# Splitting a turn of six PSUM banks into four and two in a decoder kernel

## The chip, the core and the metric

The kernel runs on one core of a Trainium2 chip. [...] TensorE's results land in PSUM, which has eight banks of 128 partitions by 512 single-precision numbers. A bank can be written again only when the last reader of its old contents is done. The metric is the device time of one execution in microseconds (us): less is better.

## What is computed

The reference is one decoder layer on x of shape (4, 256, 512) with a context of shape (4, 1601, 512):

```python
x = _layernorm(x + _L0_attn_ref(x, ...))        # attention over the 16 head dimensions, per position
x = _layernorm(x + _L0_xattn_ref(x, context))   # cross attention, most of the work
x = _layernorm(x + _L0_ffn_ref(x, ...))         # softmax router, top 8 of 64, mixes expert biases

def _L0_xattn_ref(latents, context, Wq, Wk, Wv, Wo, q_norm_w, k_norm_w):
    kv = concatenate([context, latents], axis=1)           # 1601 + 256 rows
    q, k, v = latents @ Wq, kv @ Wk, kv @ Wv               # 32 query heads, 8 key/value heads, 128 wide
    q, k = rms_norm(q, q_norm_w), rms_norm(k, k_norm_w)
    probs = softmax(q @ k.T / sqrt(128))                   # 4 query heads share one key/value head
    return concat(probs @ v) @ Wo
```

## The kernel before

**Precision.** Each large operand is kept as a high and a low half-precision part, and each product is three matmuls: high by high, high by low, low by high (`mm3`, lines 229 to 235; the three matmuls are lines 233, 234 and 235).

**Tiling.** The 1857 rows of keys and values of a sequence lie in 15 tiles of 128 (the last has 65 rows), taken in eight pairs. A unit is one key/value head of one sequence: 8 heads by 4 sequences give 32 units, and sequence 0's eight units come first. A unit has four query heads, so there are 128 heads in all. The text calls such a query head a head, and its place in the schedule is a number: head n stands at n.

**One unit.** `kv_proj` (line 382) projects one pair onto keys and values, 24 matmuls into one PSUM bank named `kvp`. ACT squares the keys and sums the squares (line 395), POOL turns the sums into factors (397, 398), ACT and DVE make the high and low part of the values (403, 404). Later `kv_n` (408) reads the same bank again to scale the keys (ACT 418, DVE 420), which ends the bank's use, and `kv_tr` transposes the keys with a transfer. `q_proj` (432) does the same for the queries of one row tile, four heads at once, into a bank named `qp`; `q_n` (447, DVE line 451) ends its use. All this is done for the next unit while the four heads of the present one are worked through:

- `qk` (476): six matmuls make one bank `s` of scores. ACT copies it out (490), DVE takes a running maximum from it (494, 496, 499).
- `qmax`, `qmax_t`, `qmax_b`: maximum over all keys, through a bank of its own (`mt`).
- `soft` (532): for each of four chunks, DVE subtracts the maximum (537), ACT makes the exponential twice, in half and in single precision (540, 541), POOL subtracts the two for the low part (542). Eight buffers hold scores, five hold probabilities.
- `pv` (544): probabilities by values, lines 561 to 563, into one accumulator bank `o`.
- `oevac` (566): DVE and ACT empty that bank (571, 578, 580).
- `wout` (597): product with Wo into a bank `wo`, added to the result by DVE (608).

**Banks.** Six of the eight banks are one pool, `psu` (line 75), for `s`, `kvp`, `qp`, `wo` and all other matmul outputs and transposes of single-precision tiles; the maximum (`psm`) and the accumulator (`psv`) have one each.

**Order.** The opening, up to the keys and queries of the first two units, is a list written out by hand, `START` (line 29): `load`, `make`, `keep` are the context's load, its transposition and split, and its copy to memory; `proj`, `norm`, `turn` are the steps of a pair for units 0 and 1 both; `qproj`, `qnorm`, `qturn` those of unit 0's queries; `a0`, `a1`, `x0`, `x1` the steps of the first attention layer's two row tiles; `lw1`, `w1` its weights; `wkv`, `wkw`, `lwq`, `wq` weights of the second layer, `skv`, `skw`, `sq` their copies. From line 699 on every step gets a position, mostly a multiple of head numbers plus a constant from the table `AT` (line 38), and the steps are emitted by position. So `exp` and `exps` place the four chunks of `soft`, `evac` places `oevac` after a head's first `pv`, and `norm` and `turn` place `kv_n` and `kv_tr` after `kv_proj`, in parts of one tenth of the unit. Units 0 to 7 also split and save their weights (`wprep`); between sequences there are the first layer of the next one (`stage1`) and the router stage of the last one (`stage3`).

The tile framework then plans each engine's queue at compile time: it takes the emitted order as priority, and where a step's inputs or its bank would not be ready in its plan, later steps of the same engine go first. A bank of a pool is given to whichever tile the plan has next. The trace shows it: among 1108 allocations between 490 and 2322 us, 177 began while the tile six allocations earlier still held its bank.

Of the kernel before, what the change touches and what calls it, by code (L numbers as in the profile page):

```python
# [10 lines left out]
F32 = mybir.dt.float32  # L11
# [4 lines left out]
PSUM = bass.MemoryType.PSUM  # L16
DRAM = bass.MemoryType.DRAM

P = 128
# [7 lines left out]


START = """
    a0 x0 lw1 load1 w1 make1 load0 wkw wkv make0 x1 load2 a0 lwq2 a0 keep0 load3 a0 proj0 a1 norm0 a1 proj1 a1  # L30
    norm1 load4 turn1 make2 a1 load5 proj2 make3 norm2 proj3 turn0 lwq0 a0 keep1 load7 a0 norm3 a1 skv a0 a1
    make4 a1 a1 proj4 keep3 turn2 wq0 keep2 a0 make5 make7 a0 keep5 proj5 proj7 norm4 a1 wq2 turn4 make6 skw
    qproj0 norm7 qnorm0 norm5 keep6 qproj1 keep7 keep4 turn5 turn3 qturn0 proj6 qnorm1 sq qturn1 turn7 norm6
    turn6
"""


AT = dict(maxt=0.13, maxb=0.229, exp=0.327, exps=0.2, pv=2.184, pvs=-2.469, evac=1.148, out=3.37, wout=4.006, wouts=-0.187,
          qk=-0.206, qmax=-0.269, norm=0.859, turn=1.093, lead=2.991, span=3.805, z0=2, z1=1, wkv=7.932, wq=5.971,
          wqs=0.513, wq1=4.753, wo0=3.105, wo=0.635, bkv=9.366, bq=5.482, bo=3.236, lq1=2.103, l1lo=-1.004,  # L40
          l1b=-24.402, l1w=-1.49, srcl=0.764, mklo=1.584, mkb=-23.779, mke=-2.064, mktl=-1.781, prep3=3.694, s3=5.382,
          s3i=-0.465, s3w=3.874, s3l=-0.111, s3lw=0.484, lw1=2.586, lw2=3.64, lmaxt=0.127, lmaxb=0.286, lexp=0.335,
          lexps=0.178, lpv=2.055, levac=1.151, lout=3.348, lqk=1.003, lqkw=0.833)

@with_exitstack
def tile_decoder(ctx: ExitStack, tc: tile.TileContext, x, cx, Wq1, bq1, Wk1, bk1, Wv1, bv1,
# [9 lines left out]
    G = Wq.shape[1] // Wk.shape[1]  # L56
# [15 lines left out]
    pS = ctx.enter_context(tc.tile_pool(name="pS", bufs=8))  # L72
    pP = ctx.enter_context(tc.tile_pool(name="pP", bufs=5))
    dr = ctx.enter_context(tc.tile_pool(name="dr", bufs=1, space=DRAM))
    psu = ctx.enter_context(tc.tile_pool(name="psu", bufs=6, space=PSUM))
    psm = ctx.enter_context(tc.tile_pool(name="psm", bufs=1, space=PSUM))
    psv = ctx.enter_context(tc.tile_pool(name="psv", bufs=1, space=PSUM))

# [150 lines left out]
    def mm3(dst, quads, start=True, stop=True, skip=False):  # L229

        n = len(quads)
        for k, (ah, al, bh, bl) in enumerate(quads):
            nc.tensor.matmul(dst, ah, bh, start=start and k == 0, stop=False, skip_group_check=skip)  # L233
            nc.tensor.matmul(dst, ah, bl, start=False, stop=False, skip_group_check=skip)  # L234
            nc.tensor.matmul(dst, al, bh, start=False, stop=stop and k == n - 1, skip_group_check=skip)  # L235
# [4 lines left out]
    def wprep_kv(h):  # L240
        s = pst.tile([P, NC, 2 * P], F32, tag="st", name=f"st_kv_{h}")
        nc.sync.dma_start(out=s[:, :, 0:P], in_=Wk[:, h * P:(h + 1) * P].rearrange("(c p) d -> p c d", p=P))
        nc.sync.dma_start(out=s[:, :, P:], in_=Wv[:, h * P:(h + 1) * P].rearrange("(c p) d -> p c d", p=P))
        w = Wt["kv", h] = p2.tile([P, 2, NC, 2 * P], F16, tag="wkv", name=f"wkv_{h}")
        split(w[:, 0], w[:, 1], s, WS)
        if h >= HB:
            wsave("kv", h)
# [52 lines left out]
    def nk(t):  # L300
        return REM if t == NT - 1 else P

    def kview(tile_, t):

        o = (t % 2) * 2 * NC * P
        return tile_[:, o:o + 2 * NC * P].rearrange("p (l c k) -> p l c k", l=2, c=NC)[:, :, :, :nk(t)]

    def tiles_of(p):
        return [t for t in (2 * p, 2 * p + 1) if t < NT]
# [72 lines left out]
    def kv_proj(u, p):  # L382
        h, b = units[u]
        wkv = Wt["kv", h]
        ts_ = tiles_of(p)
        n = len(ts_)
        k = nk(ts_[0])
        ps = psu.tile([P, 2, 2 * P], F32, tag="u", name=f"kvp_{u}_{p}")
        for j, t in enumerate(ts_):
            v = kview(kvt[u, p], t)  # L390
            mm3(ps[:k, j, :], [(v[:, 0, c], v[:, 1, c], wkv[:, 0, c], wkv[:, 1, c]) for c in range(NC)])
        ss = p2.tile([P, 2], F32, tag="kss", name=f"kss_{u}_{p}")
        kn = p2.tile([P, 2, P], F32, tag="kn", name=f"kn_{u}_{p}", bufs=2)
        for j in range(n):
            nc.scalar.activation(kn[:k, j, :], ps[:k, j, 0:P], AF.Square, accum_out=ss[:k, j:j + 1])
        rk = p2.tile([P, 2], F32, tag="krk", name=f"krk_{u}_{p}")
        nc.gpsimd.tensor_scalar(ss[:k, :n], ss[:k, :n], 1.0 / (P * QS * QS), 1e-6 * PW * PW / (QS * QS), ALU.mult, ALU.add)
        nc.gpsimd.tensor_tensor(rk[:k, :n], ss[:k, :n], mhalf[:k, :n], ALU.pow)
        v = NPAIR * u + sum(q[0] == u for q in vuse.values())
        assert v < VR or ("pv", *vuse[v - VR]) in done  # L400
        vuse[v] = (u, p)
        vh, vl = VT[u, p] = vring[v % VR]
        nc.scalar.activation(vh[:k, :n, 0:P], ps[:k, :n, P:], AF.Copy, scale=VS / PW)
        nc.vector.scalar_tensor_tensor(vl[:k, :n, :], ps[:k, :n, P:], VS / PW, vh[:k, :n, 0:P],
                                       ALU.mult, ALU.subtract)
        kns[u, p] = (kn, rk, ps)
# [25 lines left out]
    def q_proj(u, i):  # L432
        h, b = units[u]
        wq = Wt["q", h]
        ps = psu.tile([P, G, P], F32, tag="u", name=f"qp_{u}_{i}")
        v = kview(kvt[u, TL], NF + i)
        mm3(ps.rearrange("p g d -> p (g d)"), [(v[:, 0, c], v[:, 1, c], wq[:, 0, c], wq[:, 1, c]) for c in range(NC)])
        ss = p2.tile([P, G], F32, tag="qss", name=f"qss_{u}_{i}")
        qn = p2.tile([P, G, P], F32, tag="qn", name=f"qn_{u}_{i}", bufs=1)
        for g in range(G):  # L440
            nc.scalar.activation(qn[:, g, :], ps[:, g, :], AF.Square, accum_out=ss[:, g:g + 1])
        rq = p2.tile([P, G], F32, tag="qrq", name=f"qrq_{u}_{i}")
        nc.gpsimd.tensor_scalar(ss, ss, 1.0 / P, 1e-6 * PW * PW, ALU.mult, ALU.add)
        nc.gpsimd.tensor_tensor(rq, ss, mhalf[:, :G], ALU.pow)
        qns[u, i] = (qn, rq, ps)
# [182 lines left out]
    def stage3(b, i):  # L628
# [14 lines left out]
        for c in range(NC):  # L643
# [31 lines left out]
    x0 = [stage1(0, i) for i in range(NQ)]  # L675
    first = dict(x0=lambda: next(x0[0]), x1=lambda: next(x0[1]), lw1=prep1_load, w1=prep1,
                 wkv=lambda: wprep_kv(0))
    for i in range(NQ):
        first[f"a{i}"] = lambda i=i: next(x0[i], None)
        first[f"lwq{2 * i}"] = lambda i=i: wload_q(0, 2 * i)  # L680
        first[f"wq{2 * i}"] = lambda i=i: wprep_q(0, 2 * i)
        for k, f in (("qproj", q_proj), ("qnorm", q_n), ("qturn", q_tr)):
            first[f"{k}{i}"] = lambda f=f, i=i: f(0, i)
# [4 lines left out]
    for p in range(NPAIR):  # L688
        for k, f in (("load", src_load), ("make", kv_make), ("keep", lambda b, p: kv_keep(b, p, kvt[b, p]))):
            first[f"{k}{p}"] = lambda f=f, p=p: f(0, p)  # L690
        for k, f in (("proj", kv_proj), ("norm", kv_n), ("turn", kv_tr)):
            first[f"{k}{p}"] = lambda f=f, p=p: [f(u, p) for u in range(HB)]
# [14 lines left out]

    A = AT
    WOUT = A["out"] + A["wout"]
# [30 lines left out]
    for u in range(U):  # L740
        h, b = units[u]
        if u > 0:
            t0 = 4 * (u - 1)
            if u > 1:
                at(t0 - 0.01, proj_new, u)
            steps = [("kv", p) for p in range(NPAIR) if p != TL]
            z = A["z0"] if h == 0 else A["z1"]
            steps[z:z] = [("kv", TL), ("q", 0), ("q", 1)]
            if u == 1:
                steps = [("q", 0), ("q", 1)] + 8 * [("", 0)]  # L750
            step = A["span"] / len(steps)
            for k, (what, v) in enumerate(steps):
                pos = t0 + step * k
                norm, turn = min(pos + A["norm"] * step, 4 * u - 0.006), min(pos + A["turn"] * step, 4 * u - 0.005)
                if what == "kv" and u > 1:
                    at(pos - A["lead"] * step, kv_load, u, v)
                    at(pos, kv_proj, u, v)
                    at(norm, kv_n, u, v)
                    at(turn, kv_tr, u, v)
                elif what == "q":  # L760
                    at(pos, q_proj, u, v)
                    at(norm, q_n, u, v)
                    at(turn, q_tr, u, v)
# [58 lines left out]
```

## Time and profile before

| | us |
|---|---|
| median of 3 runs | 2449.8 |
| lowest and highest | 2444.4, 2451.77 |
| profiled execution | 2446.54 |
| its span, first to last instruction | 2444.8 |
| TensorE busy | 2360.6 |
| ScalarE busy | 2082.2 |
| VectorE busy | 1919.7 |
| GpSimd busy | 1500.9 |

The profile is of one execution. Busy time counts an engine's instructions without those of its sequencer. Matmuls overlap in the array, so their ends are modelled. A line of waits names the waiting engine, the tile and line it was about to write, and who released it, then the sum in us, the number of times and the longest. In groups of instructions `out<-in` names what is written and read, then partitions by elements. The granted clock of TensorE is a share of full speed.

In the trace the first matmul starts at 6.2 us, the context's first transposition at 15.06 us, the first scores of unit 0 at 88.9 us. The units of sequence 0 run to about 490 us. The last projection of keys and values ends at about 2340 us, and the rest is the last unit's heads, the output product and the router stage.

### The profile page before, as it was taken

How to read it: one execution, taken by the hardware profiler on the slowest of the kernel's cores; microseconds unless marked ns; L12 is line 12 of the kernel's file. 1: busy time of each engine (PE TensorE's matmuls, PEld its weight loads, DVE VectorE, ACT ScalarE, POOL GpSimd, SP SyncE). 2: the span in 40 equal slices, each digit the busy share in tenths (PEclk: the TensorE clock that was granted, in tenths of full speed). 3: DMA queues.
4: the chain of work that ended last, by engine and by line, in shares of the span. 5: the costliest groups of instructions: out<-in, count | busy, mean ns of one | idle time of the engine just before them, and what ended most of it. 6: DMA issues, size and time to landing. Idle time of an engine off the chain costs nothing. (4 is left out here: it accounts for less than half of the span.)

```text
span 2444.8 us, 65605 instructions
## 1 busy us (share of the span) xinstructions
PE 2360.6 (97%) x25424; PEld 2007.9 (82%) x25424; DVE 1919.7 (79%) x3748; ACT 2082.2 (85%) x4704; POOL 1500.9 (61%) x1334
## 2 busy tenths in 40 slices
PE   7799999999999999999999999999999999999996
PEld 5587788788888888888888888888888888888874
DVE  8778888888777897787778788788777778777775
ACT  4688889889889888889888898888889888889894
POOL 2357666676566666776565666576665655666563
PEclk9899999999999999999999999999999999999998
DMA  8835666556555546555445555555544443544310
GB/s 255 236 96 148 184 166 190 161 147 179 133 128 143 153 129 181 135 138 144 136 119 138 138 141 143 143 119 142 148 107 119 132 127 108 138 122 112 95 37 27
DMA packets 393073, 338.30 MB, mean 138 GB/s; under 512 B 318516, under 2 KB 328244, under 8 KB 384568
## 3 DMA queue, kind: packets, MB, share of 16 engines
q1 hardware_dynamic: 392760, 334.10, 51.4%
q8 instruction: 199, 3.26, 0.6%
q14 instruction: 114, 0.93, 0.1%
HBM read 219.46 MB, written 38.80 MB: 106 GB/s over the span
## 5 line engine op out<-in xcount | busy, mean ns | idle before, releaser
L542 POOL TENSOR_TENSOR P<-S,P 128x1024 f16<-128x1024 f32 (+1 forms) x512 | 1032.5, 2027 | 479.2 <-ACT S L541 458.4
L561 PE MATMUL o<-Vh,P 128*128 128x129 f16 (+1 forms) x3840 | 697.8, 221 | 13.6 <-DVE oh L580 7.9
L563 PE MATMUL o<-Vh,P 128*128 128x129 f16 (+1 forms) x3840 | 698.1, 221 | 3.0 <-POOL P L542 2.8
L562 PE MATMUL o<-Vl,P 128*128 128x128 f16 (+1 forms) x3840 | 697.0, 220 | 0.0
L490 ACT COPY S<-s 128x512 f32<-128x512 f32 (+1 forms) x1024 | 576.4, 606 | 97.8 <-PE s L235 91.6
L540 ACT ACTIVATE P<-S,lnps 128x1024 f16<-128x1024 f32 (+1 forms) x512 | 571.2, 1132 | 53.2 <-DVE S L537 52.0
L541 ACT ACTIVATE S<-S,lnps 128x1024 f32<-128x1024 f32 (+1 forms) x512 | 580.1, 1139 | 0.2
L537 DVE TENSOR_TENSOR S<-S,mt 128x1024 f32<-128x1024 f32 (+1 forms) x512 | 557.6, 1148 | 25.9 <-PE mt L528 25.8
L233 PE MATMUL s<-QT,KT 128*128 128x256 f16 x1920 | 525.4, 274 | 26.1 <-DVE M L496 11.8
L235 PE MATMUL s<-QT,KT 128*128 128x256 f16 x1920 | 525.6, 274 | 0.0
L234 PE MATMUL s<-QT,KT 128*128 128x256 f16 x1920 | 525.3, 274 | 0.0
L496 DVE TENSOR_TENSOR M<-s,M 128x512 f32<-128x512 f32 x640 | 439.9, 687 | 98.5 <-ACT S L490 78.8
L561 PEld LDWEIGHTS <-P 128*128 128x128 f16 (+1 forms) x3840 | 377.6, 98 | 26.9 <-DVE oh L580 5.3
L233 PE MATMUL kvp<-wkv_back,kv 128*128 128x256 f16 (+1 forms) x1440 | 392.5, 273 | 0.1
L235 PE MATMUL kvp<-wkv_back,kv 128*128 128x256 f16 (+1 forms) x1440 | 392.5, 273 | 0.0
L234 PE MATMUL kvp<-wkv_back,kv 128*128 128x256 f16 (+1 forms) x1440 | 392.5, 273 | 0.0
L562 PEld LDWEIGHTS <-P 128*128 128x128 f16 (+1 forms) x3840 | 378.7, 99 | 16.6 <-issue 5.0
L563 PEld LDWEIGHTS <-P 128*128 128x128 f16 (+1 forms) x3840 | 377.0, 98 | 5.5 <-POOL P L542 4.3
L235 PEld LDWEIGHTS <-kv 128*128 128x128 f16 (+1 forms) x2040 | 201.3, 99 | 47.0
L233 PEld LDWEIGHTS <-kv 128*128 128x128 f16 (+1 forms) x2040 | 201.3, 99 | 44.1 <-DVE M L496 2.7
L234 PEld LDWEIGHTS <-kv 128*128 128x128 f16 (+1 forms) x2040 | 201.3, 99 | 41.2 <-issue 1.8
L233 PEld LDWEIGHTS <-KT 128*128 128x128 f16 x1920 | 188.4, 98 | 45.1 <-DVE M L496 9.5
(174 smaller groups left out, 4119.9 us busy)
## 6 DMA issues: line engine op xcount, KB each, us to landing
kv<-kvd SPq DMA_DIRECT2D x210, 512.0 KB, 3.7
wq_back<-wqd SPq DMA_DIRECT2D x24, 1024.0 KB, 6.6
wo_back<-wod SPq DMA_DIRECT2D x24, 1024.0 KB, 4.9
kvd<-kvm SPq DMA_DIRECT2D x28, 512.0 KB, 3.0
cst<-in_ctx_dram SPq DMA_DIRECT2D x24, 512.0 KB, 7.5
wkv_back<-wkvd SPq DMA_DIRECT2D x24, 512.0 KB, 4.4
st_q<-in_L_xattn_Wq_dram SPq DMA_DIRECT2D x16, 512.0 KB, 6.7
wqd<-wq SPq DMA_DIRECT2D x8, 1024.0 KB, 5.7
```

The source lines that it names most:

```text
L233: nc.tensor.matmul(dst, ah, bh, start=start and k == 0, stop=False, skip_group_check=skip)
L234: nc.tensor.matmul(dst, ah, bl, start=False, stop=False, skip_group_check=skip)
L235: nc.tensor.matmul(dst, al, bh, start=False, stop=stop and k == n - 1, skip_group_check=skip)
L490: nc.scalar.copy(sv, ps[:, :m, :])
L496: nc.vector.tensor_tensor(Mx[n], ps, Mx[n], ALU.max)
L537: nc.vector.tensor_tensor(sv, sv, Mb[n].unsqueeze(1).broadcast_to([P, m, S]), ALU.subtract)
L540: nc.scalar.activation(pt[:, 0, :m, :], sv, AF.Exp, bias=lnps, scale=ES)
L541: nc.scalar.activation(sv, sv, AF.Exp, bias=lnps, scale=ES)
L542: nc.gpsimd.tensor_tensor(pt[:, 1, :m, :], sv, pt[:, 0, :m, :], ALU.subtract)
L561: nc.tensor.matmul(a[:, :P + 1], ph, v1[:k], start=t == 0 and i == 0, stop=False, skip_group_check=True)
L562: nc.tensor.matmul(a[:, :P], ph, v0[:k], start=False, stop=False, skip_group_check=True)
L563: nc.tensor.matmul(a[:, :P + 1], pl, v1[:k], start=False, stop=t == NT - 1 and i == NQ - 1, skip_group_check=True)
```

## The change

The pool `psu` shrinks from six banks to four. A new pool `psk` of two banks takes the projections of keys and values and those of queries, except the keys and values of unit 1, which are made in the opening and stay in `psu`. The order of the opening is another one, and 28 constants of the table have new values. Some of these are used nowhere or stand behind a bound that decides (`qk`, `qmax`, `l1lo`, `mklo`, `lq1`, and `wq1`, whose steps stay the first after the opening). What the others move, in heads: the four chunks of `soft` by -0.02, +0.05, +0.12 and +0.18; `oevac` by -0.21; `kv_n` and `kv_tr` by -0.04 and -0.05; `qmax_t` and `qmax_b` by +0.04 and +0.02; loads of the context's pairs for a unit (`kv_load`) by +0.15; splits of the weights of keys and values by -0.18, of queries by -0.13; the loads of the next sequence's context by -0.13; the making of its last pair by -0.38; the router stage by 0 to 2, growing over its steps.

```diff
-    a0 x0 lw1 load1 w1 make1 load0 wkw wkv make0 x1 load2 a0 lwq2 a0 keep0 load3 a0 proj0 a1 norm0 a1 proj1 a1
-    norm1 load4 turn1 make2 a1 load5 proj2 make3 norm2 proj3 turn0 lwq0 a0 keep1 load7 a0 norm3 a1 skv a0 a1
-    make4 a1 a1 proj4 keep3 turn2 wq0 keep2 a0 make5 make7 a0 keep5 proj5 proj7 norm4 a1 wq2 turn4 make6 skw
-    qproj0 norm7 qnorm0 norm5 keep6 qproj1 keep7 keep4 turn5 turn3 qturn0 proj6 qnorm1 sq qturn1 turn7 norm6
-    turn6
+    lw1 x0 load2 load1 a0 make1 w1 load0 a0 wkv wkw a0 x1 a0 make0 proj0 a1 keep0 norm0 load3 a1 a1 proj1
+    norm1 make2 skv load5 proj2 a1 make3 lwq0 turn1 proj3 load4 norm2 a0 keep1 turn0 load7 a0 lwq2 norm3 a0 a1
+    a1 make4 a1 wq0 proj4 a1 turn2 a0 keep3 keep2 make5 make7 a0 proj5 a1 proj7 norm4 wq2 skw make6 turn4
+    keep6 keep5 qproj0 qnorm0 keep4 norm5 qturn0 keep7 turn5 qproj1 turn3 proj6 sq qnorm1 norm7 norm6 turn6
+    turn7 qturn1
...
-AT = dict(maxt=0.13, maxb=0.229, exp=0.327, exps=0.2, pv=2.184, pvs=-2.469, evac=1.148, out=3.37, wout=4.006, wouts=-0.187,
-          qk=-0.206, qmax=-0.269, norm=0.859, turn=1.093, lead=2.991, span=3.805, z0=2, z1=1, wkv=7.932, wq=5.971,
-          wqs=0.513, wq1=4.753, wo0=3.105, wo=0.635, bkv=9.366, bq=5.482, bo=3.236, lq1=2.103, l1lo=-1.004,
-          l1b=-24.402, l1w=-1.49, srcl=0.764, mklo=1.584, mkb=-23.779, mke=-2.064, mktl=-1.781, prep3=3.694, s3=5.382,
-          s3i=-0.465, s3w=3.874, s3l=-0.111, s3lw=0.484, lw1=2.586, lw2=3.64, lmaxt=0.127, lmaxb=0.286, lexp=0.335,
+AT = dict(maxt=0.174, maxb=0.246, exp=0.309, exps=0.269, pv=2.184, pvs=-2.469, evac=0.935, out=3.37, wout=4.006, wouts=-0.187,
+          qk=-0.056, qmax=0.879, norm=0.729, turn=0.939, lead=2.613, span=3.814, z0=2, z1=1, wkv=8.109, wq=6.097,
+          wqs=0.453, wq1=5.643, wo0=2.924, wo=0.661, bkv=9.366, bq=5.482, bo=3.236, lq1=0.884, l1lo=2.581,
+          l1b=-24.402, l1w=-1.492, srcl=0.889, mklo=1.634, mkb=-23.779, mke=-2.068, mktl=-2.165, prep3=3.644, s3=6.05,
+          s3i=-0.084, s3w=4.91, s3l=-0.111, s3lw=0.484, lw1=2.586, lw2=3.64, lmaxt=0.127, lmaxb=0.286, lexp=0.335,
...
-    psu = ctx.enter_context(tc.tile_pool(name="psu", bufs=6, space=PSUM))
+    psu = ctx.enter_context(tc.tile_pool(name="psu", bufs=4, space=PSUM))
+    psk = ctx.enter_context(tc.tile_pool(name="psk", bufs=2, space=PSUM))
...
-        ps = psu.tile([P, 2, 2 * P], F32, tag="u", name=f"kvp_{u}_{p}")
+        ps = (psu if u == 1 else psk).tile([P, 2, 2 * P], F32, tag="u" if u == 1 else "k", name=f"kvp_{u}_{p}")
...
-        ps = psu.tile([P, G, P], F32, tag="u", name=f"qp_{u}_{i}")
+        ps = psk.tile([P, G, P], F32, tag="k", name=f"qp_{u}_{i}")
```

## The prediction

> **What bounds the kernel now.** I read the page's busy line and slices first, then TensorE's waits, then the busy time by stage, then the timeline around one projection.
>
> ```profile
> PE 2360.6 (97%) x25424; PEld 2007.9 (82%) x25424; DVE 1919.7 (79%) x3748; ACT 2082.2 (85%) x4704; POOL 1500.9 (61%) x1334
> PE   7799999999999999999999999999999999999996
> ACT  4688889889889888889888898888889888889894
> ```
>
> TensorE is the bound: 84.2 us of the 2444.8 us span are idle, and the change takes away no matmul. The table by stage (columns: busy us and instructions of each engine, clock, DMA) tells where the idle lies:
>
> ```profile
> 0.00:122.00 122.00, 90.28 (x673) 70.18 (x674) 94.63 (x174) 71.14 (x208) 33.98 (x79) 0.93 0.83 245
> 122.00:490.00 368.00, 348.88 (x3765) 295.13 (x3764) 303.76 (x549) 328.98 (x708) 236.97 (x191) 0.98 0.60 158
> 490.00:2322.00 1832.00, 1821.02 (x19934) 1563.91 (x19933) 1438.72 (x2860) 1599.86 (x3657) 1169.11 (x1026) 1.00 0.51 134
> 2322.00:2444.80 122.80, 100.39 (x1060) 78.64 (x1057) 82.55 (x168) 82.26 (x134) 60.84 (x39) 0.92 0.11 32
> ```
>
> Idle TensorE time is 31.7 us in the opening, 19.1 in the first sequence, 11.0 in the long middle and 22.4 in the tail. The middle has almost nothing to win. What TensorE waited for:
>
> ```profile
> PE s L233 <- DVE M L496: 11.8, 11, 3.0
> PE o L561 <- DVE oh L580: 7.9, 12, 1.9
> PE kvtp L340 <- DMA cst<-in_ctx_dram: 7.8, 1, 7.8
> PE x1tp L171 <- DMA xt<-in_x_dram: 6.2, 1, 6.2
> PE s L233 <- ACT S L490: 4.9, 7, 2.3
> ```
>
> The first and last lines are score tiles waiting for a bank that DVE's maximum or ACT's copy has not released. One bank's life, from ACT's timeline in the middle:
>
> ```profile
> 1306.60 1.27 ACT L541 ACTIVATE S<-S,lnps 128x1024 f32<-128x1024 f32 x1
> 1310.51 0.42 ACT L395 ACTIVATE kn<-kvp 128x128 f32<-128x128 f32 x1
> 1311.28 1.52 ACT L490 COPY S<-s 128x512 f32<-128x512 f32 x3
> 1315.36 1.29 ACT L418 ACTIVATE kh<-kvp,krk 128x128 f16<-128x128 f32 x4 [1.29 <-POOL krk L398]
> ```
>
> TensorE began this projection at 1303.75. ACT ran eight exponentials nearly back to back (1302.2 to 1310.8, one score copy at 1303.22 and two short pairs between), so its squares began only at 1310.51; the last read ended near 1316.7: a bank held 13 us.
>
> **Counts that price the banks.** I paired each bank's first matmul with the end of its last reader in the timeline. Between 490 and 2322 us a score bank is held 5.14 us on average, a projection of keys and values 12.4, of queries 11.1, an output 4.75. A head takes 18.2 us there (806 score tiles, eight to a head, in 1832 us). A unit of four heads (72.7 us) fills 32 score, 2 output, 8 + 2 projection banks. Two banks for projections would be held (8x12.4+2x11.1)/(2x72.7) = 84% of the time, four for the rest (32x5.14+2x4.75)/(4x72.7) = 60%. In the first sequence, with holds of 13.9, 13.1, 6.86 and 4.28 us and a unit of 76.5 us, it is 90% and 75%.
>
> Of the allocations 332 took the last of the six banks, and TensorE stood 26.8 us before them: 4.9 us before 13 in the ramp (85 to 122 us), 15.3 before 85 in the first sequence, 3.8 before 208 in the middle, 2.9 before 26 in the tail. On the same timeline, 313 score and output tiles would take the last of four and 269 projections the last of two: 18, 113, 420 and 31 in the four stages.
>
> **The change, part by part.**
>
> 1. *Six banks become four and two.* Per last-bank allocation the old price is 0.37, 0.18, 0.018 and 0.11 us. At these prices the new counts cost 6.8 + 20.3 + 7.7 + 3.4 = 38.2 us, so +11.3. Below: all 26.8 us of bank idle goes. Above: projections that began while two others were held would have been put off by 99.1 us (75 of them, mean 1.3), scores beyond four by 146.7 (66). Only what the planner cannot fill with other matmuls is idle; the low price of 208 tight allocations in the middle says it mostly can, so I take +11.3. [...]
>
> A bank wait has a second price. By the same table over short stretches, TensorE was busy 0.25 of the 2.2 us from 1152.0, and from 1155.6 its clock stood at 0.51 for 3.4 us: 1.7 us more per stop of 2 us. Of the 75 put-off projections 16 exceed 2 us, so this price is at most 27 us.
>
> [...]
>
> 2. *The evacuation of a head's output moves up* from 1.148 to 0.935 head after its first product, 3.9 us earlier. Its ACT and DVE instructions (two of 0.43 and two of 0.34 us a head, a reciprocal of 0.16) pass one score copy and maximum at most. The products of the next head share one accumulator bank and waited 7.9 us for this. I take -4, bounds 0 and -7.9.
>
> 3. *The four softmax chunks of a head spread out*, 0.269 head apart instead of 0.2 (4.9 us for 3.6): the first comes 0.3 us earlier, the others 0.9, 2.1, 3.3 us later. Each is a DVE subtraction (1.15), two ACT exponentials (1.14 each) and a POOL subtraction (2.03). In 3.6 us ACT gets 2.3 us of these, 1.6 score copies of 0.6 and half a projection's 2.4 (two squares, two reads of their sums, three copies): 4.5 us, a quarter too much, hence the clump above; in 4.9 us it gets 2.3 + 1.3 + 1.7 = 5.3, a tenth too much. Scores waited about 19 us for their ACT and DVE readers; a quarter gone is -5, bounds 0 and -19. The price elsewhere: the last chunk's values come at 2.116 + 5.5/18.2 = 2.42 heads and their products at 2.98, 10 us of cover; POOL, 61% busy, hides its 2 us. The five probability buffers are needed (1.10x4) 4.4 deep instead of 4.8, the eight score buffers 5.4 instead of 5.0.
>
> 4. *Start order.* SP issues the first layer's weights before x, and context pair 2 before pair 1, which TensorE needs first. Before, the first pair let TensorE go at 15.06 and the second landed at 16.4: +1.4. The rest up to the first scores (88.9 us) has some 9 us of idle between 15 and 89 to win. Sequence 0's ten projections of unit 0 on two banks (8 x 8.9 + 2 x 8.4)/2 = 44 us fit in the 68 us between 21 and 89. I take +1.4, bounds -9 and +9.
>
> 5. *The rest.* Normalisation and key transposes (two ACT, two DVE, one POOL pair, one SP transpose) come 0.8 and 1.0 us earlier, already in the bounds above as shorter holds: with every put-off 0.9 us shorter, the 99.1 us become 49.8. Loads of the context (SP) come 2.7 us later; they land in 3.7 us with a lead of 17.8, and without that cover each would stop TensorE for its own 3.7. Weight preparation comes 2 to 3 us earlier: loads on SP, 1.1 us splits on ACT, 1.2 to 1.4 on DVE; unit 1's move passes nothing, since nothing stands between the two places. The router stage starts up to a head later and spreads over more: DVE's small steps get thinner. All at zero, bounds -3 and +3 (0.9 us waits before its statistics are in the trace).
>
> Sum: 11.3 - 4 - 5 + 1.4 = +3.7 on the profiled execution's 2446.5 us (1.7 around its span). The median, 2449.8, lies 3.3 above it, so I add 3.3: **2453 us**.
>
> **Rivals.**
>
> *Two banks make projections wait (slower).* For: 84 and 90% occupancy, a reuse distance of one projection, long holds when ACT clumps. Against: TensorE hardly ever waited before projections (1.1 us over 96 last-bank ones). It decides once half of the 49.8 us become idle: 24.9 us, with five half-clock stretches 8.5, in place of part 1's 11.3: 2453 + 22.1 = 2475. Below a third it drowns in the forecast.
>
> *The bank idle goes (faster).* For: 26.8 us hang on banks, mostly scores, and scores no longer share a turn with 13 us holds; chunks no longer clump. Half of it gone, -13.4, and -6 from part 2 give 2430.
>
> *Four banks starve the ramp and the tail (slower).* No projection needs the other two after about 2340 us, and five or six banks were held for scores in 77% of the ramp and 55% of 2322 to 2380. One put-off of 13.6 us, the ramp's longest, is exposed: 13.6 less the 1.9 counted gives 2465. Against: ACT and DVE set the pace there, not the depth.
>
> *It does nothing.* The planner reorders TensorE to match, and scores and outputs held more than four banks in only 0.2% of the middle, projections more than two in 4%: 2450, the median of before.
>
> **How the numbers follow.** A kernel of this spread is told from no change at about 0.3%, 7.3 us. The forecast has 0.38, its own range 2441 to 2465 (its terms' uncertainty): same 0.22, slower 0.11, faster 0.05. Projections wait 0.25 (slower), idle goes 0.27 (faster), ramp and tail 0.05 (slower), nothing 0.05 (same). So faster 0.32, same 0.27, slower 0.41. The outer rivals, 2430 and 2475, may themselves miss by half their term; 2426 to 2484 leaves some 2 in 10 out.
>
> **What the profile after would show.** Part 1: TensorE's waits before kvp and qp on L420 and L451, and more half-clock stretches, if the rival holds; near zero if not. Part 2: the wait of o on L580 shrinks from 7.9. Part 3: copies between exponentials on ACT. Part 4: first kvtp near 16.4 us. Ramp and tail: idle above 31.7 and 22.4. Wrong would be an idle in the middle above 30 us, or an opening and first sequence below 35 together.

## The result and the profile after

The changed kernel takes 2480.9 us (median of 4 runs, 2476.12 to 2482.85) against 2448.42 for the kernel before in the same comparison: 1.0136 times as long, 95% interval 1.0122 to 1.0149, or some 32 us more. The profiled execution's span grew from 2444.8 to 2480.1 us. The forecast of 2453 was 28 us too low; 2481 lies inside the range given (2426 to 2484), near its upper end, which was set by the rival in which two banks make the projections wait (2475). Lines of the new file stand one further down: the score and projection matmuls are lines 234 to 236, the key normalisation on DVE is 421, the maximum 497.

In the pages PE is TensorE, PEld the loading of its weights, DVE VectorE, ACT ScalarE and POOL GpSimd; SP, SyncE, issues the transfers. The page after, busy line and TensorE's slices and clock:

```profile
PE 2367.1 (95%) x25424; PEld 2007.8 (81%) x25424; DVE 1907.1 (77%) x3748; ACT 2085.6 (84%) x4704; POOL 1507.9 (61%) x1334
PE   6889999999999999999999999999999999999986
PEclk9999999999999999999999999999999999999997
```

No engine got more work, and the granted clock stayed at nine tenths or more until the last slice. TensorE's idle rose from 84.2 to 113.0 us; the other 6.5 us of the longer span are in its busy time. Stretches at half clock sum to 69.5 us of the span after and 57.0 before; the 12.5 us more, at half the rate, are an estimated 6 us of it. By stage (columns as before):

```profile
122.00:490.00 368.00, 342.49 (x3706) 290.88 (x3704) 302.55 (x543) 325.12 (x678) 235.53 (x180) 0.97 0.58 154
490.00:2322.00 1832.00, 1801.76 (x19646) 1541.06 (x19645) 1412.53 (x2827) 1583.59 (x3607) 1157.93 (x1013) 1.00 0.51 134
```

In the 1832 us of the middle TensorE did 19646 matmuls where it had done 19934, and stood 30.2 us instead of 11.0. What it waited for there, first the kernel before, then the changed one (columns: us in total, times, longest):

```profile
PE o L561 <- DVE oh L580: 4.9, 5, 1.9
PE s L233 <- ACT S L490: 2.1, 4, 0.9
PE s L233 <- DVE bnmv L154: 1.5, 2, 0.9
```

```profile
PE kvp L234 <- DVE kh L421: 11.0, 14, 2.1
PE s L234 <- DVE M L497: 6.7, 9, 2.2
PE o L562 <- DVE oh L581: 1.7, 2, 1.4
```

A wait that did not exist is now first: a projection that cannot start because an earlier one, in one of the two banks, has not been normalised. The waits before scores grew as well. All waits before `kvp` sum to 12.0 us in the middle (0 before), before `s` to 11.7 (4.6 before). That a bank is written again only after its last reader shows best where there is one: at each of the 127 turns of `o` the first matmul began 52 ns or more after the last reader of the head before had ended, in both traces.

**Where the time went.** Since TensorE is the bound and its matmuls are the same, two runs can be laid side by side at equal work. I took a matmul's work as its columns at 2.4 per ns plus 3 ns, which fits the distance between starts in the trace before (medians 109 ns at 256 columns, 57 at 129, 216 at 512; the record of one with 256 lasts 273 ns, so they overlap). Single-precision columns are counted four times; that weight is my estimate and was not shown (in the median 128 of them took 109 ns, 128 in half precision 56), but it is the same in every run. Lost is the time by which a matmul's start lies beyond the work done before it. All of it is some 2344 us, the same in every run. Lost beyond the kernel before, in us, up to 700 us of work (the opening and sequence 0), from 700 to 2250, and after that:

| run | up to 700 | 700 to 2250 | the rest | span |
|---|---|---|---|---|
| changed kernel (four banks, and two for projections) | +5.1 | +22.6 | +7.6 | +35.3 |
| tables6 (new opening and table, six banks) | +16.2 | -1.6 | +0.7 | +15.3 |
| opening6 (new opening alone, six banks) | +11.5 | -1.7 | +1.3 | +11.2 |
| soft6 (two parts of the table, six banks) | -1.0 | -2.0 | 0.0 | -3.0 |
| split_old (four and two, old opening and table) | +12.0 | +26.2 | +4.4 | +42.7 |
| q_in_four (changed kernel, queries back to the four) | +12.2 | +30.1 | +2.1 | +44.4 |
| three_three (three banks and three) | +45.0 | +53.9 | +13.5 | +112.4 |
| five_one (five banks for scores, keys and values; one apart) | +21.5 | +4.9 | +1.2 | +27.7 |
| norm_early (normalisation placed earlier) | +8.1 | +24.0 | +8.0 | +40.1 |
| tail_k (last unit's scores on all six banks) | +5.3 | +22.1 | +0.3 | +27.7 |
| const_norm (keys scaled by a constant) | +14.5 | -0.7 | +7.1 | +21.0 |

These are single profiled executions, so a few us either way mean little; the ratios below come from timed runs.

### The profile page after: what moved, and what is told of

The parts are those of the page before. It is cut to its first block, busy times and chain, and to the rows that moved or that the text cites. A ratio compares the mean times of both kernels' runs of the same rounds, so it can differ in the third digit from the quotient of the medians.

```text
span 2480.1 us, 65590 instructions
## 1 busy us (share of the span) xinstructions
PE 2367.1 (95%) x25424; PEld 2007.8 (81%) x25424; DVE 1907.1 (77%) x3748; ACT 2085.6 (84%) x4704; POOL 1507.9 (61%) x1334
## 5 line engine op out<-in xcount | busy, mean ns | idle before, releaser
L234 PE MATMUL kvp<-wkv_back,kv 128*128 128x256 f16 (+1 forms) x1440 | 394.3, 274 | 11.5 <-DVE kh L421 11.3
```

## The experiments

Three theories stood: (1) projections hold a bank too long for a turn of two; (2) the new order and constants cost the time; (3) the partition as such does, because four or two banks cannot lend to each other.

### The pools and the tables, one at a time

The changed kernel's opening and table on six banks, for all projections too:

```diff
-    psu = ctx.enter_context(tc.tile_pool(name="psu", bufs=4, space=PSUM))
-    psk = ctx.enter_context(tc.tile_pool(name="psk", bufs=2, space=PSUM))
+    psu = ctx.enter_context(tc.tile_pool(name="psu", bufs=6, space=PSUM))
```

> The new opening and the new table, all on the old pool of six banks. If the turn of two for projections is the cause (theory 1), the tables alone cost nothing: 2440 to 2455 us, and TensorE waits at most 2 us before kvp on the key normalisation, as before. If the new order and constants are the cause (theory 2), it stays near 2481. If the four banks for scores are the cause (theory 3), it is also 2440 to 2455, and the runs with other splits tell.

Measured: 2461.98 us, 1.0064 times before (1.0049 to 1.0079). No theory had this: the tables cost 15 us on six banks, all of it before 700 us of work and none in the middle.

The changed kernel's four and two banks under the `START` and `AT` of the kernel before (the two tables as the change's diff shows them, taken back):

```diff
-    lw1 x0 load2 load1 a0 make1 w1 load0 a0 wkv wkw a0 x1 a0 make0 proj0 a1 keep0 norm0 load3 a1 a1 proj1
+    a0 x0 lw1 load1 w1 make1 load0 wkw wkv make0 x1 load2 a0 lwq2 a0 keep0 load3 a0 proj0 a1 norm0 a1 proj1 a1
...
```

> The four and two banks under the old opening and the old table. Theory 1 (turn of two): the keys are normalised 0.8 us later than under the new table, so the waits before projections are at least those of the changed kernel (17 us) and the time is 2480 to 2500. Theory 2 (order and constants): near 2449. Theory 3 (four banks for scores): near 2480, with the loss before s and not before kvp.

Measured: 2491.55 us, 1.0187 (1.0170 to 1.0204). So the split is what costs the middle (+26.2 us there), and the new tables take back some 10 us of its price. TensorE's waits before `kvp` on the normalisation and on the queries were 17.5 us, as theory 1 expected; theory 3 had expected the loss before `s` and none there. The pieces don't add: 15 for the tables and 45 for the split make 60, and together they cost 32. Up to 700 us of work the old tables lost 0 on six banks and 12 on the split, the new ones 16 and 5.

The new opening alone, in the kernel before, tells which table it was:

```diff
-    a0 x0 lw1 load1 w1 make1 load0 wkw wkv make0 x1 load2 a0 lwq2 a0 keep0 load3 a0 proj0 a1 norm0 a1 proj1 a1
+    lw1 x0 load2 load1 a0 make1 w1 load0 a0 wkv wkw a0 x1 a0 make0 proj0 a1 keep0 norm0 load3 a1 a1 proj1
...
```

> The new order of the opening alone, on six banks with the old table. The new opening and table together cost 15 us on six banks, all of it before 400 us of TensorE's work were done. If the opening does it: 2458 to 2466, lost time 8 us more than before already at 80 us of work. If the table does it: 2445 to 2451.

Measured: 2459.42 us, 1.0055 (1.0038 to 1.0072). The new opening is nearly all of the 15 us. Its loss was 7.6 us at 80 us of work and 10.2 at 400, near what was expected of it.

### Parts 2 and 3 of the prediction by themselves

In the kernel before:

```diff
-AT = dict(maxt=0.13, maxb=0.229, exp=0.327, exps=0.2, pv=2.184, pvs=-2.469, evac=1.148, out=3.37, wout=4.006, wouts=-0.187,
+AT = dict(maxt=0.13, maxb=0.229, exp=0.309, exps=0.269, pv=2.184, pvs=-2.469, evac=0.935, out=3.37, wout=4.006, wouts=-0.187,
```

> The kernel before with two parts of the new table alone: softmax chunks 0.269 head apart and the output's evacuation at 0.935. By the prediction's parts 2 and 3 it gains 9 us: 2438, with the wait of o on the evacuation (7.9 us) halved and the waits of s on its readers down by a quarter. If these are what cost time in the table on six banks: 2455 to 2463. If neither matters: 2444 to 2451.

Measured: 2446.54 us, 1.0001 (0.9991 to 1.0010, 10 runs): nothing. The waits of the whole run say why:

```profile
PE s L233 <- DVE M L496: 15.0, 14, 3.0
PE o L561 <- DVE oh L580: 5.8, 10, 1.9
```

The wait on the evacuation fell from 7.9 to 5.8 us, half of the expected gain, and the one of scores on DVE's maximum rose from 11.8 to 15.0. A score bank in the middle was held 5.23 us on average (5.14 before): spreading the exponentials did not shorten the holds, which is what the gain was to come from.

### Which side of the partition is short

Three banks each:

```diff
-    psu = ctx.enter_context(tc.tile_pool(name="psu", bufs=4, space=PSUM))
-    psk = ctx.enter_context(tc.tile_pool(name="psk", bufs=2, space=PSUM))
+    psu = ctx.enter_context(tc.tile_pool(name="psu", bufs=3, space=PSUM))
+    psk = ctx.enter_context(tc.tile_pool(name="psk", bufs=3, space=PSUM))
```

> The changed kernel with three banks for projections and three for everything else. Theory 1: the waits before kvp and qp (19 us in the changed kernel) fall below 4 us; if scores were indifferent the time would fall to about 2460. Theory 3: scores on three banks lose more than on four, and the time rises above 2490, with the waits before s above the 33 us of the changed kernel. Theory 2: 2481.

Measured: 2559.42 us, 1.0463 (1.0447 to 1.0478). Three and three are far worse than four and two. The longest waits:

```profile
PE s L234 <- DVE M L497: 39.2, 41, 3.4
PE o L562 <- DVE oh L581: 23.2, 23, 2.7
PE kvp L234 <- DVE kh L421: 15.5, 12, 2.7
```

The third line is a miss for theory 1: with a third bank the projections were expected to wait under 4 us. The trace shows that the holds did not stay what they were: a projection of keys and values held its bank 17.3 us on average in the middle, against 12.2 in the changed kernel, so the third bank bought little. Why the holds grew is not shown; my guess is that a stall of TensorE before scores, 39.2 us in 41 stops there on the maximum alone, also delays what ACT and DVE get.

Queries back to the pool of four:

```diff
-        ps = psk.tile([P, G, P], F32, tag="k", name=f"qp_{u}_{i}")
+        ps = psu.tile([P, G, P], F32, tag="u", name=f"qp_{u}_{i}")
```

> The changed kernel with the queries' projections back in the pool of four, so that two banks take only keys and values: occupancy of the two falls from (8x12.2+2x11.8)/(2x72.7) = 83% to 67%, that of the four rises from 60 to about 68%. Theory 1: waits before kvp fall from 17 us to under 8, time 2460 to 2472. Theory 3: the four get fuller, time 2485 or more. Theory 2: 2481.

Measured: 2491.77 us, 1.0182 (1.0162 to 1.0203).

```profile
PE s L234 <- DVE M L497: 27.2, 25, 2.5
PE kvp L234 <- DVE kh L421: 4.0, 5, 1.4
```

Relieving the two banks removed most of the wait before projections (on the normalisation 4.0 us over the whole run, 12.6 in the changed kernel) and put more than that before the scores (on the maximum 27.2, 16.0 there). The four are short as well, as theory 3 says. Here too the holds grew, to 13.8 us for keys and values.

Five shared and one apart:

```diff
-    psu = ctx.enter_context(tc.tile_pool(name="psu", bufs=4, space=PSUM))
-    psk = ctx.enter_context(tc.tile_pool(name="psk", bufs=2, space=PSUM))
+    psu = ctx.enter_context(tc.tile_pool(name="psu", bufs=5, space=PSUM))
+    psk = ctx.enter_context(tc.tile_pool(name="psk", bufs=1, space=PSUM))
...
-        ps = (psu if u == 1 else psk).tile([P, 2, 2 * P], F32, tag="u" if u == 1 else "k", name=f"kvp_{u}_{p}")
+        ps = psu.tile([P, 2, 2 * P], F32, tag="u", name=f"kvp_{u}_{p}")
...
-        ps = psk.tile([P, G, P], F32, tag="k", name=f"qp_{u}_{i}")
+        ps = (psk if u else psu).tile([P, G, P], F32, tag="k" if u else "u", name=f"qp_{u}_{i}")
...
-            wps[u, i] = tps(f"wo_{u}_{i}")
+            wps[u, i] = psk.tile([P, 512], F32, tag="k", name=f"wo_{u}_{i}")
```

> The changed kernel with another partition: five banks shared by scores and the projections of keys and values, one bank for the queries from unit 1 on and the output product. The five would be held (32x5.3+8x12.2)/(5x72.7) = 73% of the time, the one 45%. If lost sharing is the cause (theory 3), most of the sharing is back and the loss in the middle (22 us between 700 and 2250 us of TensorE's work) falls below 10: 2462 to 2472. If the turn of the long projections is the cause (theory 1), they now sit among five banks as among six before: 2460 to 2470 as well, with no wait before kvp; the queries on one bank would show their own waits. If both fail, 2481 or more.

Measured: 2475.33 us, 1.0121 (1.0106 to 1.0137). In the middle the loss was 4.9 us instead of 22.6, as both theories expected, and TensorE stood 0.5 us before `kvp` there. The wait of queries on their one bank did not show. The total missed the expected 2462 to 2472, because sequence 0 and the opening lost 21.5 us; a likely reason, not tested, is that the opening was written for four and two banks. So the cost in the middle grows with how much sharing is lost: about 0 with six shared, 5 with five and one, 23 to 30 with four and two, 54 with three and three.

### How long a projection holds its bank

Normalising earlier by priority:

```diff
-          qk=-0.056, qmax=0.879, norm=0.729, turn=0.939, lead=2.613, span=3.814, z0=2, z1=1, wkv=8.109, wq=6.097,
+          qk=-0.056, qmax=0.879, norm=0.45, turn=0.66, lead=2.613, span=3.814, z0=2, z1=1, wkv=8.109, wq=6.097,
```

> The changed kernel with the key and query normalisation 0.28 of a step earlier (norm 0.45, turn 0.66 instead of 0.729, 0.939), about 1.9 us. If the length of a projection's hold makes the two banks too few (theory 1), the mean hold of 12.2 us in the middle falls by 1 to 2 us, TensorE's waits before kvp there (12.0 us in the changed kernel) fall below 6, and the time falls to 2465 to 2476. If the loss comes from a partition as such, whichever side is short (theory 3), the earlier work only moves the wait to the scores: within 5 us of 2481.

Measured: 2484.23 us, 1.0152 (1.0137 to 1.0168), no better than the changed kernel. The experiment did not do what it was to do: the mean hold in the middle stayed at 12.3 us (12.2 in the changed kernel). The earlier place in the order moved nothing. In both runs the factor, which needs the squares on ACT and GpSimd's power, was ready 7.7 us after a projection's first matmul on average, and ACT began to scale the keys at 10.1 us, 2.4 us later. So the chain is most of the hold, but not all.

Copying the keys out of the bank:

```diff
+        kc = p2.tile([P, 2, P], F32, tag="kc", name=f"kc_{u}_{p}", bufs=2)
+        nc.vector.tensor_copy(kc[:k, :n, :], ps[:k, :n, 0:P])
...
-        kns[u, p] = (kn, rk, ps)
+        kns[u, p] = (kn, rk, kc)
```

> The changed kernel with one more DVE copy per projection (256 elements a row, about 0.4 us, 100 us of DVE time in all) that takes the keys out of the bank, so that the normalisation reads SBUF and the bank is free about 7 us after its first matmul instead of 12.2; occupancy of the two banks falls from 83% to about 55%. Theory 1 (projections held too long for two banks): TensorE's waits before kvp in the middle fall from 12.0 to under 4 us and the time to 2462 to 2472. Theory 3 (the partition, whichever side): kvp waits fall but s and o waits rise by as much through the busier DVE, 2478 to 2490.

Measured: 2555.9 us, 1.0451 (1.0434 to 1.0469). Neither theory expected this, and it decides nothing between them, for the normalisation itself became slower. The hold fell only to 11.3 us, not to the 7 that were meant. The group in that run, then the same instructions in the kernel before (min/median/max in ns):

```profile
L423 DVE SCALAR_TENSOR_TENSOR kh<-kc,krk,kh x480: 260/347/2526, 33.8 to 2445.5; 128x128 f16<-128x128 f32 x159, 65x128 f16<-65x128 f32 x1
```

```profile
L420 DVE SCALAR_TENSOR_TENSOR kh<-kvp,krk,kh x480: 260/344/361, 32.0 to 2348.5; 128x128 f16<-128x128 f32 x159, 65x128 f16<-65x128 f32 x1
```

The median is nearly the same, the longest is seven times as long: see the last section. On six banks the same copy was to gain:

> The kernel before, six banks, with the same early copy of the keys out of the bank. TensorE stood 26.8 us before allocations that took the last bank; banks freed 5 us earlier by each projection should remove most of the 3 to 5 us in the middle and a part of the 15 us in the first sequence, where DVE is 83% busy and gets 0.4 us more per projection: 2435 to 2448. If DVE's extra work counts more than the banks: 2450 to 2465.

Measured: 2532.65 us, 1.0353 (1.0338 to 1.0369), for the same reason: the normalisations of 128 rows took 681 ns on average, 345 in the kernel before.

Another way to shorten the hold is to take the wait out of it, by leaving out the normalisation of the keys:

```diff
-            nc.scalar.activation(kh[:k, j, 0, :], ps[:k, j, 0:P], AF.Copy, scale=rk[:k, j:j + 1])
+            nc.scalar.activation(kh[:k, j, 0, :], ps[:k, j, 0:P], AF.Copy, scale=0.139)
...
-            nc.vector.scalar_tensor_tensor(kh[:k, j, 1, :], ps[:k, j, 0:P], rk[:k, j:j + 1], kh[:k, j, 0, :],
+            nc.vector.scalar_tensor_tensor(kh[:k, j, 1, :], ps[:k, j, 0:P], 0.139, kh[:k, j, 0, :],
...
-          qk=-0.056, qmax=0.879, norm=0.729, turn=0.939, lead=2.613, span=3.814, z0=2, z1=1, wkv=8.109, wq=6.097,
+          qk=-0.056, qmax=0.879, norm=0.0, turn=0.939, lead=2.613, span=3.814, z0=2, z1=1, wkv=8.109, wq=6.097,
```

> The changed kernel with the scaled keys made at once, right after the projection, by a constant in place of the row's factor: the same instructions on every engine, but they no longer wait for the squares' sums and GpSimd's power. It leaves out the normalisation of the keys (the factors are computed and not used; the queries' factors are, with their scaling placed earlier). A projection's bank should be free some 8 to 9 us after its first matmul instead of 12.2, occupancy of the two banks about 60%. Theory 1 (projections held too long for a turn of two): waits before kvp in the middle fall from 12.0 to under 4 us, the loss there from 22 us to under 8, time 2455 to 2468. Theory 3 (the partition, whichever side is short): four banks for scores still lose, at least half of the 22 us stays, 2470 to 2482.

Measured: 2467.71 us, 1.0093 (1.0076 to 1.0110), at the edge of what theory 1 expected; the waits before `kvp`, 5.3 us, missed its 4. The waits in the middle:

```profile
PE kvp L234 <- DVE kh L421: 3.9, 7, 1.3
PE s L234 <- DVE M L500: 3.6, 1, 3.6
PE kvp L234 <- DVE qn L452: 1.4, 3, 0.6
```

The mean hold fell from 12.2 to 10.4 us, less than the 8 to 9 that were meant, the waits before `kvp` from 12.0 to 5.3, those before `s` from 11.7 to 6.0, and the middle's whole loss of 22.6 us was gone (-0.7). ACT now began to scale the keys 8.7 us after a projection's first matmul instead of 10.1, although nothing but the projection itself, over at 2.9 us, fed it: much of the hold is not that chain. ACT's other work and the two buffers for scaled keys are what is left, and were not told apart. So with holds two microseconds shorter four and two banks do suffice there, although theory 3 expected at least half to stay. The opening and sequence 0 lost 14.5 us instead of 5.1. One reserve: an immediate factor also makes the two instructions shorter (ACT 395 to 336 ns, DVE 343 to 283), 37 and 30 us of engine time, so the gain is not that of the wait alone. The same edit on six banks was not run, so the two are not told apart. Taken together, the split costs the middle (split_old against the kernel before), relieving one side makes the other wait (q_in_four), and shorter holds undo the loss (const_norm, with that reserve).

### The tail

```diff
-        ps = psu.tile([P, 2, S], F32, tag="u", name=f"s_{n}_{p}")
+        own = u == U - 1 and p % 2
+        ps = (psk if own else psu).tile([P, 2, S], F32, tag="k" if own else "u", name=f"s_{n}_{p}")
```

> The changed kernel, where the last unit takes every second score tile from the two projection banks, which nothing else uses by then: six banks for scores again in the tail. The tail (after 2280 us of TensorE's work) cost 7.6 us more than before the change. If four banks for scores are the reason, 2472 to 2476; if it is the order, 2481.

Measured: 2471.97 us, 1.0103 (1.0085 to 1.0121), 8 us less than the changed kernel by the two ratios. The loss after 2250 us of work is gone (7.6 to 0.3) and the middle is as it was (22.1). Four banks for scores were the reason in the tail.

No version was faster than the kernel before; soft6 is its equal.

## Why the prediction was right or wrong

**The bound: right. The place of the loss: not.** TensorE stayed the bound, and the middle had almost nothing to win. But it had much to lose: from 700 us of work on it took 22.6 of the 35 us, where the sum gave it 3.9 of its 11.3 (7.7 less 3.8). The forecast named an idle above 30 us in the middle, or below 35 in the opening and first sequence together, as signs of being wrong. The first came, at 30.2; the second did not (55.3). That 2481 still lies in the range is owed to the margin around the rival, not to the sum.

**Part 1, the banks: right in kind, mis-sized, above all in the middle.** In the ramp, sequence 0, middle and tail the sum had 6.8, 20.3, 7.7 and 3.4 us before allocations that take the last bank. The trace after shows 6.1, 15.9, 21.7 and 5.4, at 13, 108, 469 and 26 allocations. That is 49.1 us where the sum had 38.2, and 22.3 more than the 26.8 before, out of 28.8 us of new idle. The counts held (18, 113, 420, 31); the price of one in the middle was 0.046 us, not 0.018. The step that failed is taking the price from six shared banks. My reading, which no run isolates: there a tile may get any of six, and a late release of one costs nothing, while with two few releases help. The rival had the mechanism and, at 2475, nearly the size. Its condition was that half of the 49.8 us of put-offs falls idle; 19.1 us stood before projections in the whole run, 38%, and the waits before scores, 7 us longer in the middle than before, and the tail's 7.6 us did their part.

**Half-clock stretches: too many expected.** The rival had five more; the middle had 3 instead of 2, each 3.4 us long with a granted clock of 0.50. The longest wait before a projection there was 2.1 us; it ended at 1936.5 us, and no half-clock stretch followed until 2045.3. Each of the three came after 3.4 us in which TensorE had been busy for 1.1 to 1.8 us. Even three_three, with 54 us more lost in the middle, had only 7 half-clock stretches there, 27 us at half clock against 7 in the kernel before, which is an estimated 10 of the 54 us.

**Part 2 (-4) and part 3 (-5): wrong.** Together they measured 0 in soft6. Part 2's wait did shrink by 2.1 us; part 3's step, that exponentials further apart shorten the score holds, failed (5.23 us after 5.14).

**Part 4, the opening (+1.4): one time nearly right, the sum unclear.** The first context transposition came at 15.88 us (15.06 before; 16.4 was expected). But with the first layer's weights issued before x, the first matmul of all came at 13.3 us instead of 6.2, which the sum did not have, and the first scores at 96.2 instead of 88.9:

```profile
PE x1tp L172 <- POOL b L148: 13.3, 1, 13.3
```

On six banks the new opening costs some 13 us, outside the bounds of 9; on the split the whole stretch up to 700 us of work cost 5.1 with the new tables and 12.0 with the old. What the new opening does on the split alone was not run.

**Part 5: the shorter hold failed.** Normalising 0.8 us earlier was to shorten every hold by 0.9 us. In the middle the mean went from 12.41 to 12.15 us; in the first sequence it rose, from 13.9 to 16.2. norm_early shows that the place in the order is not what sets it.

**Ramp and tail:** 13.6 us was expected of the rival, mainly from the ramp; the tail alone cost 7.6, and the ramp's bank waits rose only from 4.9 to 6.1 us.

**What stays open.** Why const_norm frees the scores too is argued, not shown: fewer stalls before projections keep ACT and DVE fed on time. Why holds grow when the pools are cut otherwise (17.3 us in three_three) is open too; the order that the planner chose there was not taken apart.

## What to carry to other kernels

A shared pool of buffers is worth more than the mean occupancies say: 84% and 60% looked affordable for two and four banks, and cost 22 us in the middle that six shared banks did not. The likely reason is that a planned order meets late releases, which a larger choice of buffers absorbs. A price taken from a shared pool does not carry over to its parts, nor do its hold times. Before splitting a pool, shorten the long holders by what they wait for (here in part a chain over GpSimd), not by their place in the order. An order that suits one pool can cost time on another (some 13 us for the new opening on six banks): try each half of such a change alone.

## What the hardware showed

In free_early the key normalisations on DVE, with both tensor inputs in SBUF (`kc` and `kh`), took longer when GpSimd was at work. Of 480, 150 began while GpSimd's subtraction of the probabilities ran; they took 1481 ns on average, when that subtraction had 1360 ns left, so they ended on average 121 ns after it. The 263 that began while GpSimd did nothing took 367 ns. In the kernel before, with one input in PSUM, 229 began during the same subtraction and took 345 ns; none of the 480 took over 361. So the normalisations took 360 us of DVE time instead of 165, beside some 100 us for the copies themselves; with both, the runs grew by 75 us on the split and 86 on six banks. What held them up is not shown.

The scaling of the keys with a factor from a column of SBUF instead of the instruction took 59 ns more on average on ACT and 60 on DVE at 128 elements (395 against 336, 343 against 283, changed kernel against const_norm). The shortest on ACT were 97 ns apart (347 and 250).
